# Attention weights asked for among the expert blocks, two blocks turned together, and a new order of work where the experts hand over to self attention

## The chip, the cores and the metric

The kernel runs on one core of one Trainium2 chip. The metric is device time in microseconds for one execution, the median of several runs. All of the work is one launch.

## What is computed

A decoder of two layers for `B = 4` sequences of `S = 512` rows of `D = 256`, with a context of `S2 = 1601` rows for each sequence. After each of its six parts the row is normalized again:

```python
x = _layernorm(x + _L0_attn_ref(x, ...))              # a per-token gradient step, run as attention
x = _layernorm(x + _L0_xattn_ref(x, ctx, ctx, mask, ...))
x = _layernorm(x + _L0_ffn_ref(x, Wr, br, Wi, bi, Wg, bg, Wo, bo, gamma, beta))
x = _layernorm(x + _L1_attn_ref(x, w_qkv, w_out))     # 16 heads of 16, causal
x = _layernorm(x + _L1_xattn_ref(x, ctx, ctx, mask, ...))  # 16 heads, keys and queries turned (rope)
x = _layernorm(x + _L1_ffn_ref(x, ...))               # quantized weights, F = 1024
```

The change touches the third part and the beginning of the fourth. The third is a mixture of `E = 8` experts: for each row the best two of the eight (by `softmax(x @ Wr + br)`) compute

```python
h = gelu(xf @ Wi_e + bi_e) * sigmoid(xf @ Wg_e + bg_e)      # 256 -> 1024
r = xf + (h @ Wo_e + bo_e)                                  # 1024 -> 256
y_e = (r - mu) * rsqrt(var + EPS) * g_e + b_e
```

and the row's result is the sum of its two `y_e` with their weights. The cross attention of the second layer takes turned keys from the context: `K = ctx @ Wk.T + bk`, then `K * cos + swapped(K) * sin`.

## The kernel before

**Engines and order.** TensorE (PE) does the matmuls and the transposes; ScalarE (ACT) does activations and copies out of PSUM; VectorE (DVE) adds, multiplies and reduces; GpSimd (POOL) does a part of the turning, memsets and the indirect DMAs; SyncE (SP) has no arithmetic and issues most DMAs. From the experts on, the program is under a manual schedule (L1146, L1173): each engine carries out its instructions in the order in which the Python code emits them, and an instruction that waits holds all behind it on its engine, a DMA issue too.

**Experts.** Just before the experts, values of the cross attention of the last two sequences are computed and written to the DRAM arrays `vd` (L790 to L794, ACT). The routing scatters each row, normalized, into a DRAM array `xs`, sorted by expert. The rows are computed in blocks of 256: one first block for each of the eight experts (`"first"`, static addresses), and blocks of what is left (`"more"`, two halves of 128 rows, each with an expert found at run time). They run in the order `"ffmfmmfmfmmfmfmmf"` and two more `"m"` (L1138). For one block:

- `rows_of` (L918) loads its 256 rows, `xb`: on SP for a first block (L922, 256 KB), by two indirect DMAs on POOL for another (L928). There are three `xb` buffers.
- `turned` (L933) makes four transposes on PE (L939) and copies them with DVE to `xbT` (L943).
- `first_half` (L946) multiplies by `eWi` (32 matmuls), then by `eWg` (32), with gelu and sigmoid on ACT (L975) and their product on DVE (L977). Between its quarters it asks for `eWi` and `eWg` of the next block: on SP for a first block (L407, 1028 KB each), on POOL for another (L409). There are two buffers of each.
- `second_half` (L982) multiplies by `eWo`, normalizes on DVE (`rb`), writes `ys` (L1012, SP), asks for the rows of the block after the next, and through `outs` for a later `eWo`.

`run` (L1105) strings these together: it asks for the rows of two blocks (`rows_of(b)` for `blocks[:2]`), for the first `eWo`, turns the first block, and then for each block `i`: `first_half(i)`, `turned(i + 1)`, `second_half(i - 1)`, which asks for the rows of `i + 2`. `eWi` and `eWg` of the first two blocks were loaded long before.

**Loads for the attention.** Ahead of all that, L896 to L901 ask for eight weights of 256 KB and four small rows and columns, on SP. In the program they stand in front of `run`, so in SP's queue they stand in front of the first `xb<-xs`. More loads are a generator, `attention_first` (L1019): `run` takes one step of it behind each block. Its steps, in order: masks for the self attention (`c_diagq`, `c_later`, on ACT); context of the first sequence into `qt` and `ks` tiles (L1034, ACT); cosine and sine tables (L1044, ACT); three steps of constant rows written to the DRAM arrays `qd`, `ksd`, `kcd` behind their data (`behind`, L876, ACT; `kcd<-c_rowkc` is the third); memsets on POOL; then four steps that load a piece of the mask on SP (`mi`, L1066), turn it into an addend on DVE (`mf`, L1070) and write it on SP to `mrow` (L1071); `masked(0)` (L879, ACT) copies `mrow` to `kcd[0]`; last come small products of weights (L1091 and after).

**From the experts to the self attention.** In the stage that begins at L1173, emission order again is the order on each engine. The tiles of this stage lie where those of the experts lay; the first load into them is `ln_gamma` (L1575, SP). `combined(b)` returns lists of steps: `fetch` gathers each row's two `ys` rows by indirect DMAs on POOL (L1224); `add` adds them on DVE (L1238) and normalizes the rows, with a root on ACT and an apply; `turn` transposes the rows on PE (L1254) and copies them to `xT` on ACT (L1257). Then `self_rows(b, c)` computes, for half of the heads, k and q (L1271, L1273): a matmul group, an eviction on ACT, a write on SP to `ksd` or `qd` (`to_rows`, L1203), and, in a separate step (`rows0`), the loads of `ks` and `qt` by head groups (`from_rows`, L1206). `self_values` (L1283) computes the values. `context(b, keys, values)` computes keys (`key`, L1325) and values (`value`, L1341) of the cross attention: a key is a matmul group with `xaK`, an eviction on ACT to `raw` (L1332), the turning of `rotated` (L1294; a shuffle on DVE L1298, and three operations on DVE or POOL L1299 to L1301) and a write on SP to `kcd`. There are four `raw` buffers. Values of the second sequence, `values1`, need context chunks `cx`, which `chunk` asks for (L1316, SP, two buffers) one ahead.

The order at this seam was written out by hand at L1773 to L1784: four keys of the first sequence (matmul and eviction, with turning and writing put off to `turns0`), then `add`, then `turns0` (four times turning and writing), three values, `turn`, k and q, `rows0`, four self values, six more values. While these run, `all_banks` is truthy and `one()` (L1187) hands out seven PSUM banks. Behind them the units of the attention start: `slot1` (L1386) computes scores and their row maxima, `subtracted` (L1447) takes the maximum off the queries, `scores` (L1460), `exponents` (L1472) and `weighted` (L1484) follow, with other work (`extras`, `starts`) put between them: `extras[0]` begins with k and q of the second half of the heads, then more keys.

Of the kernel before, what the change touches and what calls it, by code (L numbers as in the profile page):

```python
# [12 lines left out]
AF = mybir.ActivationFunctionType  # L13
# [26 lines left out]
def decoder(ctx: ExitStack, tc: tile.TileContext, a: dict, out: bass.AP):  # L40
    nc = tc.nc
# [33 lines left out]
    def weight(pool, name):  # L75

        src = a[name]
        t = pool.tile([P, 2, src.shape[1]], F32, tag=name, name=name)
        nc.sync.dma_start(t, src.rearrange("(c p) n -> p c n", p=P))
        return t  # L80
# [134 lines left out]
    with (  # L215
# [15 lines left out]
        ps = wide()  # L231
# [661 lines left out]

    with tc.tile_pool(name="p3", bufs=2) as p3, ExitStack() as ordered:
        W = {}
        for name in ("qkvQ", "qkvK", "xaQ", "xaK", "qkvV", "xaV", "outP", "xaO"):  # L896
            W[name] = weight(plw, name)
        bqc = column(plw, "bq")
        bkc = column(plw, "bk")
        bvc = column(plw, "bv")  # L900
        bo_x = row(plw, "xa_bo")  # L901

# [114 lines left out]
        def attention_first():  # L1019

            ready["diagq"] = const(p4a, "c_diagq", [P, 896], nc.scalar)

            later = p3.tile([P, 2 * P], F32, tag="c_later", name="c_later", bufs=1)
            nc.scalar.dma_start(later, a["c_later"])
            ready["later"] = p4a.tile([P, 2 * P], BF16, tag="later", name="later")
            yield
            nc.gpsimd.tensor_copy(ready["later"], later)
            qt, ks = ready["qt"], ready["ks"] = [group_tiles(p4a, n, S) for n in ("qt", "ks")]

            at = qt + ks  # L1030
            for i, k0 in enumerate(range(0, S2, 512)):
                kw = min(512, S2 - k0)
                for h in range(2):
                    nc.scalar.dma_start(at[2 * i + h][:, :kw], a["ctxT"][0, h * P : (h + 1) * P, k0 : k0 + kw])  # L1034
            yield

            for i, k0 in enumerate(range(0, S2, 512)):
                kw = min(512, S2 - k0)
                if i < B - 1:
                    pair = [xT[1 + i][:, h, :] for h in range(2)]  # L1040
                else:
                    pair = [p4a.tile([P, kw], F32, tag=f"turn{h}", name=f"turn{h}") for h in range(2)]
                for t, name in zip(pair, ("c_cos", "c_sin")):
                    nc.scalar.dma_start(t, a[name][:, k0 : k0 + kw])  # L1044
                ready["turn", i] = pair
            yield
            behind(qd[0], "c_rowq")
            behind(ksd[0], "c_rowks")
            yield
            behind(kcd[0], "c_rowkc")  # L1050
            yield
            ngs = ready["ngs"] = []
            for i in range(2 * NT):
                t = p4a.tile([P, 4, 32], F32, tag=f"ng{i}", name=f"ng{i}")
                nc.gpsimd.memset(t, 0.0)
                ngs.append(t)
            ready["vself"] = [values_tile(p4a, f"vs{i}", NT) for i in range(2)]
            yield


            any_ = p3.tile([4 * B, 4], F32, tag="any", name="any", bufs=1)
            for c, k0 in enumerate(range(0, S2, 401)):
                kw = min(401, S2 - k0)
                mi = p3.tile([4 * B, 401], I32, tag="mi", name="mi", bufs=1)[:, :kw]
                for b in range(B):
                    nc.sync.dma_start(  # L1066
                        mi[4 * b : 4 * b + 4, :], a["mask"][b, k0 : k0 + kw].partition_broadcast(4)
                    )
                mf = p3.tile([4 * B, 401], F32, tag="mf", name="mf", bufs=1)[:, :kw]
                nc.vector.tensor_scalar(mf, mi, 0.0, MASKED, ALU.is_equal, ALU.mult)  # L1070
                nc.sync.dma_start(mrow[:, k0 : k0 + kw], mf)  # L1071
                nc.vector.tensor_reduce(any_[:, c : c + 1], mf, AX.X, ALU.max)
                yield
            masked(0)
            yield
            left = p3.tile([4 * B, 1], F32, tag="left", name="left", bufs=1)
            nc.vector.tensor_reduce(left, any_, AX.X, ALU.max)
            nc.vector.tensor_scalar(left, left, 0.0, QS, ALU.is_equal, ALU.mult)
            ones16 = p3.tile([4 * B, P], F32, tag="ones16", name="ones16", bufs=1)
            nc.gpsimd.memset(ones16, 1.0)  # L1080
            dia = p3.tile([4 * B, 4 * B], F32, tag="dia", name="dia", bufs=1)
            nc.vector.tensor_scalar(dia, ident[: 4 * B, : 4 * B], left, None, ALU.mult)
            yield
            ps = bank()
            mm(ps[:, : 4 * B], [(ones16, dia)])
            nc.vector.tensor_copy(live, ps[:, : 4 * B])
            for b in range(B):
                nc.vector.tensor_scalar(liveb[:, b, :], bqc, live[:, 4 * b : 4 * b + 1], None, ALU.mult)
            yield

            ps = bank()  # L1091
            mm(ps[0:1, :D], [(bvc[:, c : c + 1], W["xaO"][:, c, :]) for c in range(2)])
            nc.vector.tensor_tensor(bo_x, bo_x, ps[0:1, :D], ALU.add)
            yield
            ps = bank()
            mm(ps[:, :D], [(ones, bo_x)])
            nc.vector.tensor_copy(bob, ps[:, :D])
# [7 lines left out]
        def run(blocks, work):  # L1105

            get = lambda i: blocks[i] if i < len(blocks) else None
            for b in blocks[:2]:
                rows_of(b)
            for name in ("eWi", "eWg"):  # L1110
                for h in range(2):
                    if (blocks[0], name) not in first_loads:
                        weights_of(blocks[0], name, h)

            ahead = [(b, h) for b in blocks for h in range(len(halves(*b)))]
            taken = [0]

            def outs(free):
                taken[0] -= free
                while ahead and taken[0] < 3:  # L1120
                    b, h = ahead.pop(0)
                    weights_of(b, "eWo", h)
                    taken[0] += 1

            outs(0)
            turned(blocks[0])
            for i, b in enumerate(blocks):
                first_half(b, get(i + 1))
                if get(i + 1):
                    turned(get(i + 1))  # L1130
                if i:
                    second_half(blocks[i - 1], get(i + 2), outs)
                elif get(2):
                    rows_of(get(2))
                next(work, None)
            second_half(blocks[-1], None, outs)
# [30 lines left out]
    with ExitStack() as s4:  # L1167
# [143 lines left out]
        def chunk(n):  # L1311
            while len(chunk_tiles) < min(n + 2, len(stream)):
                b, c = stream[len(chunk_tiles)]
                k0, kw = chunks[c]
                t = p4.tile([P, 2, 512], F32, tag="cx", name="cx", bufs=2)
                nc.sync.dma_start(  # L1316
                    t[:, :, :kw], a["ctxT"][b].rearrange("(c p) k -> p c k", p=P)[:, :, k0 : k0 + kw]
                )
                chunk_tiles.append(t)
            return [chunk_tiles[n][:, h, :] for h in range(2)]  # L1320

        def context(b, keys, values, here=None):


            def key(src, i, c, eng, apart=None):  # L1325
                if apart is None:
                    flush(1)
                k0, kw = chunks[i]
                ps = one()
                mm(ps[:, :kw], [(W["xaK"][:, h, c * P : (c + 1) * P], src()[h][:, :kw]) for h in range(2)])  # L1330
                raw = raw_tile()
                nc.scalar.activation(raw[:, :kw], ps[:, :kw], AF.Identity, bias=bkc[:, c : c + 1])  # L1332
                turn = lambda: rotated(raw, kw, slice(k0, k0 + kw), eng, ready["turn", i] if here else None)
                write = lambda: to_rows(kcd[b], c, k0, kw, raw[:, :kw])
                if apart is None:
                    turn()
                    going.append(write)
                else:
                    apart.append(lambda: (turn(), write()))
# [430 lines left out]
        )  # L1770
        (k1_, q1_), rows1 = self_rows(0, 1)
        turns0 = []
        for f in keys0[0:2] + keys0[4:6]:  # L1773
            f(turns0)
        for f in add + turns0 + values1[:3] + turn + [k0_, q0_, rows0] + self_values(0) + values1[3:9]:
            f()
        all_banks.clear()
        cosT = const(p4c, "c_cos", [P, S2], nc.sync)
# [2 lines left out]

        extras[0] = [
            k1_, q1_, *keys0[2:4], lambda: (keys0[6](), keys0[7]()), lambda: (flush(0), rows1()),
            *values1[9:11],  # L1784
        ] + extras[0]
        extras[1] = values1[11:] + keys1[:2] + extras[1]
        for i, n in enumerate((2, 5)):
# [245 lines left out]
```

## Time and profile before

| | |
|---|---|
| runs, us | 2396.34, 2378.8, 2392.78 |
| median of the runs, us | 2392.78 |
| profiled execution, us | 2391.23 |
| its span, us | 2389.1 |
| mean granted TensorE clock | 0.971 |
| busy, us: PE, PEld, DVE, ACT, POOL | 2270.9, 1287.5, 1231.9, 1063.0, 369.3 |
| instructions | 36156 |
| read from HBM, written, MB | 196.12, 56.77 |

The profile is of one execution. "PEld" is the loading of weights into TensorE, which runs beside the matmuls. In the slices each digit is the busy share of a fortieth of the span in tenths, and PEclk is the granted clock of TensorE. Lines with PE, SPq and so on give start, duration, engine, source line and operation; "SPq", "ACTq" and "POOLq" are issues of DMAs by these engines, "x4" is a count, and square brackets hold the idle time before and what ended it. Lines of waits give the sum, the count and the longest. Rows of windows give the length and then, for each engine, busy time and number of instructions; the last three numbers are the granted clock, the busy share of the DMA engines and GB/s.

### The profile page before, as it was taken

The numbers are of one execution on the slowest core, as the hardware profiler recorded it, in microseconds if no ns is written. First come the engines' busy times: TensorE is split into PE (matmuls) and PEld (weight loads), VectorE is DVE, ScalarE is ACT, GpSimd is POOL, SyncE is SP. The second block draws the span as 40 slices with busy tenths as digits, with TensorE's granted clock in tenths as the row PEclk, the third lists the DMA queues.
The fourth block names the chain that finished last, engine by engine and source line by source line (L and its number), as shares of the span: only waits on it lengthen the run. The fifth ranks groups of instructions, "written<-read, shape, count | busy, mean of one in ns | idle before, by whom it ended". The sixth has DMA issues, their size and how long they took to land.

```text
span 2389.1 us, 36156 instructions
## 1 busy us (share of the span) xinstructions
PE 2270.9 (95%) x14448; PEld 1287.5 (54%) x14448; DVE 1231.9 (52%) x2918; ACT 1063.0 (44%) x2103; POOL 369.3 (15%) x383
## 2 busy tenths in 40 slices
PE   7899999977999999879999999999999999999998
PEld 4768577756888988633333334333333333333366
DVE  1433334431333434455656667666766776777234
ACT  1111222223554645424555443655656565666730
POOL 1010001130222122335230010211112010000000
PEclk9999999988999999989999998999999999999999
DMA  8400311135887767352221310112110010100000
GB/s 302 177 0 1 133 55 46 46 126 190 333 307 269 291 260 297 108 173 85 67 87 54 116 37 1 38 33 72 63 39 28 25 60 15 64 1 21 29 9 27
DMA packets 77099, 244.13 MB, mean 102 GB/s; under 512 B 11640, under 2 KB 34686, under 8 KB 64638
## 3 DMA queue, kind: packets, MB, share of 16 engines
q1 hardware_dynamic: 60126, 141.96, 17.2%
q0 software_dynamic: 13632, 89.32, 9.9%
q10 hardware_dynamic: 3168, 10.48, 1.2%
q8 instruction: 116, 1.90, 0.3%
q14 instruction: 57, 0.47, 0.1%
HBM read 196.12 MB, written 56.77 MB: 106 GB/s over the span
## 4 chain that ended last, share of the span: by engine, by line
PE 53%; ACT 1%; DVE 1%; DMA 1%; POOL 1%; issue 0%; SPq 0%; DVEq 0%; ACTq 0%; POOLq 0%
PE s L1467 23%; PE one L202 12%; PE po L1494 12%; PE s L202 3%; PE s L1477 1%; PE one L1452 1%; PE one L1515 1%; DMA cx<-in_ctxT 1%; ACT x L171 1%; DVE one L1426 0%; ACT ex L1481 0%; DMA y<-ys,yrows 0%; DVE pm L1424 0%; PE one L1536 0%; DMA qd<-q 0%
## 5 line engine op out<-in xcount | busy, mean ns | idle before, releaser
L1481 ACT ACTIVATE ex<-s 128x512 f32<-128x512 f32 (+1 forms) x1062 | 578.0, 594 | 465.5 <-PE s L1467 225.3
L1424 DVE TENSOR_REDUCE pm<-one 128x1 f32<-128x512 f32 x768 | 492.8, 685 | 161.1 <-PE s L1467 106.1
L1467 PE MATMUL s<-q,kc 32*128 32x512 f32 x1612 | 528.8, 639 | 0.8 <-ACT ex L1481 0.8
L202 PE MATMUL one<-kc,qt 32*128 32x512 f32 (+1 forms) x2048 | 483.5, 563 | 0.3 <-DVE pm L1424 0.3
L1467 PEld LDWEIGHTS s<-q,kc 32*128 32x128 f32 x1612 | 166.1, 179 | 203.1 <-issue 170.0
L1494 PE MATMUL po<-ex,v 128*32 128x256 f32 (+3 forms) x2688 | 251.5, 443 | 0.3 <-ACT ot L1507 0.3
L1426 DVE CUSTOM_DVE_ANT_0 one<-one,c_diagq 128x512 f32<-128x512 f32 x256 | 171.9, 715 | 97.8 <-PE one L202 88.2
L1494 PEld LDWEIGHTS po<-ex,v 128*32 128x32 f32 (+1 forms) x2688 | 54.1, 108 | 253.1 <-issue 246.4
L1467 PE MATMUL s<-q,ks 32*128 32x512 f32 x512 | 180.6, 658 | 6.2 <-ACT ex L1481 4.9
L202 PEld LDWEIGHTS one<-kc,qt 32*128 32x128 f32 x2048 | 164.5, 188 | 11.8 <-DVE pm L1424 7.4
L202 PE MATMUL bank<-eWo,g 128*128 128x256 f32 x608 | 140.3, 387 | 11.5 <-DVE rb L997 8.2
L202 PE MATMUL one<-ks,qt 32*128 32x512 f32 x512 | 149.6, 664 | 0.0
L202 PE MATMUL wide<-xbT,eWi 128*128 128x128 f32 (+1 forms) x960 | 141.0, 308 | 4.0 <-DVE xbT L943 4.0
L977 DVE TENSOR_TENSOR g<-g,sg 128x1024 f32<-128x1024 f32 x38 | 46.4, 1224 | 180.3 <-ACT sg L975 171.9
L202 PEld LDWEIGHTS wide<-xbT,eWi 128*128 128x128 f32 x960 | 131.1, 194 | 13.4 <-issue 4.2
L202 PE MATMUL wide<-xbT,eWg 128*128 128x128 f32 (+1 forms) x960 | 137.0, 303 | 0.0
L202 PEld LDWEIGHTS bank<-eWo,g 128*128 128x128 f32 x608 | 115.5, 194 | 31.0 <-DVE rb L997 12.2
L1299 POOL TENSOR_TENSOR raw<-raw,c_cos 128x512 f32<-128x512 f32 (+1 forms) x32 | 35.0, 1093 | 626.5 <-DVE swp L1298 626.5
L202 PEld LDWEIGHTS wide<-xbT,eWg 128*128 128x128 f32 x960 | 128.1, 191 | 6.6
L1467 PEld LDWEIGHTS s<-q,ks 32*128 32x128 f32 x512 | 53.4, 187 | 83.9 <-issue 64.6
L975 ACT ACTIVATE g<-wide,eWi 128x128 f32<-128x128 f32 (+1 forms) x240 | 72.6, 410 | 56.8 <-PE wide L202 56.4
L202 PE MATMUL wide<-ctxT,q 128*128 128x512 f32 (+1 forms) x256 | 91.3, 510 | 0.8 <-DVE q L669 0.8
(346 smaller groups left out, 2948.5 us busy)
## 6 DMA issues: line engine op xcount, KB each, us to landing
xs<-zero SPq DMA_DIRECT2D x32, 512.0 KB
kc<-kcd SPq DMA_DIRECT2D x16, 800.5 KB
eWo<-in_eWo SPq DMA_DIRECT2D x8, 1408.0 KB
eWi<-in_eWi SPq DMA_DIRECT2D x8, 1028.0 KB
eWg<-in_eWg SPq DMA_DIRECT2D x8, 1028.0 KB
qt<-qd SPq DMA_DIRECT2D x32, 256.0 KB
ctxT<-in_ctxT SPq DMA_DIRECT2D x4, 1601.0 KB
cx<-in_ctxT SPq DMA_DIRECT2D x12, 512.0 KB
```

What stands on the lines that cost most here:

```text
L171: nc.scalar.activation(into(t), xb[:, t, :], AF.Identity, scale=mid["rs"][:, t : t + 1], bias=mid["nb"][:, t : t + 1],)
L202: nc.tensor.matmul(ps, l, r, start=(i == 0), stop=(i == n - 1))
L975: nc.scalar.activation(dst[:, k, :], pv[:, k, :], func, bias=bias)
L977: nc.vector.tensor_tensor(part, part, dst, ALU.mult)
L1299: eng.tensor_tensor(raw[:, :n], raw[:, :n], cos[:, :n], ALU.mult)
L1424: nc.vector.tensor_reduce(pm[:, t, j, c : c + 1], ps, AX.X, ALU.max)
L1426: nc.vector.tensor_tensor_reduce(out=ps, in0=ps, in1=diagq[:, 384 - t * P : 896 - t * P], scale=1.0, scalar=LOWEST, op0=ALU.add, op1=ALU.m ...
L1452: nc.tensor.transpose(pt[:, t * P : (t + 1) * P], ng.rearrange("p j r -> p (j r)"), ident)
L1467: nc.tensor.matmul(ps[:kn], kt[rows, k * P : k * P + kn], q2[rows, :], start=True, stop=cross)
L1477: nc.tensor.matmul(ps[:, k * P : (k + 1) * P], later_[:, :P], later_[:, P:], start=False, stop=True)
L1481: nc.scalar.activation(ex[:kn, h, :], ps[:kn], AF.Exp)
L1494: nc.tensor.matmul(state["po"][j * 32 : j * 32 + 32, q0:q1], (vals if cross else vself)[b % 2][:kn, k, c0 : c0 + 32], ex[:kn, j % 2, q0:q1 ...
```

## The change

The loads of the attention weights leave the place in front of the experts. They are put into two steps of the generator: four weights and the small loads at the start of its second step, four weights at the start of its seventh, ahead of the first piece of the mask. The names `bqc`, `bvc` and `bo_x` are bound there.

```diff
         W = {}
-        for name in ("qkvQ", "qkvK", "xaQ", "xaK", "qkvV", "xaV", "outP", "xaO"):
-            W[name] = weight(plw, name)
-        bqc = column(plw, "bq")
-        bkc = column(plw, "bk")
-        bvc = column(plw, "bv")
-        bo_x = row(plw, "xa_bo")
+
+        def attention_weights(names):
+            for name in names:
+                W[name] = weight(plw, name)
...
             ready["later"] = p4a.tile([P, 2 * P], BF16, tag="later", name="later")
             yield
+            attention_weights(("xaV", "xaK", "qkvK", "qkvQ"))
+            for name in ("bq", "bk", "bv"):
+                ready[name] = column(plw, name)
+            ready["xa_bo"] = row(plw, "xa_bo")
             nc.gpsimd.tensor_copy(ready["later"], later)
...
             ready["vself"] = [values_tile(p4a, f"vs{i}", NT) for i in range(2)]
             yield
+            attention_weights(("qkvV", "xaQ", "outP", "xaO"))
+            bqc, bvc, bo_x = (ready[k] for k in ("bq", "bv", "xa_bo"))
```

The first two blocks are turned one after the other, ahead of the first block's matmuls; until now the second was turned behind the first half of the first:

```diff
             outs(0)
-            turned(blocks[0])
+            for b in blocks[:2]:
+                turned(b)
             for i, b in enumerate(blocks):
                 first_half(b, get(i + 1))
-                if get(i + 1):
+                if i and get(i + 1):
                     turned(get(i + 1))
```

At the seam, two of the four keys precede `add` and a third follows it; then come the transposes of `x`, k and q, the fourth key, and the loads of the finished rows. Turning and writing of the four keys stand behind all of these. Eight values follow instead of nine, the ninth going to `extras[0]`. The context chunks asked for meanwhile go to ACT's queue:

```diff
-                nc.sync.dma_start(
+                (nc.scalar if all_banks else nc.sync).dma_start(
                     t[:, :, :kw], a["ctxT"][b].rearrange("(c p) k -> p c k", p=P)[:, :, k0 : k0 + kw]
                 )
...
-                nc.scalar.activation(raw[:, :kw], ps[:, :kw], AF.Identity, bias=bkc[:, c : c + 1])
+                nc.scalar.activation(raw[:, :kw], ps[:, :kw], AF.Identity, bias=ready["bk"][:, c : c + 1])
...
         turns0 = []
-        for f in keys0[0:2] + keys0[4:6]:
-            f(turns0)
-        for f in add + turns0 + values1[:3] + turn + [k0_, q0_, rows0] + self_values(0) + values1[3:9]:
+        apart = lambda f: lambda: f(turns0)
+        order = [apart(f) for f in keys0[0:2]] + add + [apart(keys0[4])] + turn + [k0_, q0_, apart(keys0[5]), rows0]
+        for f in order:
+            f()
+        for f in turns0 + self_values(0) + values1[:8]:
             f()
         all_banks.clear()
...
-            *values1[9:11],
+            *values1[8:11],
```

No arithmetic is added or left out.

## The prediction

> **What bounds the kernel now.** I read the slices first, then what TensorE (PE) waits for, then the two places where it stops.
>
> ```profile
> PE   7899999977999999879999999999999999999998
> PEclk9999999988999999989999998999999999999999
> DMA  8400311135887767352221310112110010100000
> ```
>
> A slice is 59.7 us. PE is full nearly everywhere, so the end is set by PE's work plus its holes. Two dips lie at the stages that the diff touches: slices 9 and 10 (experts begin) and 17 and 18 (experts end, attention begins). The waits of PE in 545:600 and in 1000:1040 name both:
>
> ```profile
> PE bank L939 <- DMA xb<-xs: 19.0, 1, 19.0
> PE wide L202 <- DVE xbT L943: 4.0, 2, 3.2
> PE one L202 <- DMA cx<-in_ctxT: 11.3, 1, 11.3
> ```
>
> The timeline of the first hole (start, duration, engine, line; brackets: idle before, and what ended it):
>
> ```profile
> 531.37 0.37 SPq L79 DMA_DIRECT2D qkvQ<-in_qkvQ  x1
> 542.89 1.08 SPq L922 DMA_DIRECT2D xb<-xs  x2
> 546.00 1.09 PE L939 MATMUL bank<-ident,xb 128*128 128x128 f32 x4 [18.98 <-DMA xb<-xs]
> 547.92 9.06 PE L202 MATMUL wide<-xbT,eWi 128*128 128x256 f32 x32 [0.84 <-DVE xbT L943]
> 567.50 8.83 PE L202 MATMUL wide<-xbT,eWi 128*128 128x256 f32 x32 [3.17 <-DVE xbT L943]
> 576.17 7.07 PE L202 MATMUL wide<-xbT,eWg 128*128 128x256 f32 x32
> ```
>
> SP is free at 531.37, but issues twelve attention loads before the rows that PE waits for. And the second:
>
> ```profile
> 1013.07 9.37 SPq L1203 DMA_DIRECT2D kcd<-raw  x4
> 1022.55 0.58 SPq L1203 DMA_DIRECT2D ksd<-q  x1
> 1028.95 0.34 SPq L1206 DMA_DIRECT2D qt<-qd  x1
> 1030.34 0.93 SPq L1316 DMA_DIRECT2D cx<-in_ctxT  x2
> 1036.51 2.05 PE L202 MATMUL one<-xaV,cx 128*128 128x256 f32 x4 [11.30 <-DMA cx<-in_ctxT]
> 1038.49 2.06 PE L202 MATMUL one<-ks,qt 32*128 32x512 f32 x8
> ```
>
> SP holds the finished k and q behind four writes of turned keys (9.4 us); the next context chunk, which PE's order has ahead of the first scores, stands behind both.
>
> **Experts begin.** The first xb load takes the place of qkvQ. In the built order it waits for the same things (the vd writes, behind which qkvQ went at 531.37) and the last scatter (issued 519.27, long done). So it issues at 531.4. Its landing is the row's 546.00 - 542.89 = 3.1 us: PE starts at 534.5. Both blocks are turned, 2 x 1.1 at the clock of that place; the first expert matmul comes at 536.7 instead of 547.92: **-11.2**. Unknown is the landing of the second xb, beside POOL's eWo (issued 532.26): 2 to 5 us for both, so -9 to -12. Then, before the second block, the turn (0.6) and the wait for its DVE copy (3.17) go: **-3.8**.
>
> The third part is the clock, and here a rule is weighed. Two-us rows of the granted clock (the column behind the engines):
>
> ```profile
> 550.00:552.00 2.00, 2.00 (x6) 1.61 (x6) 0.00 (x0) 0.00 (x0) 0.00 (x0) 0.56 1.00 408
> 552.00:554.00 2.00, 2.00 (x11) 1.76 (x10) 0.00 (x0) 0.43 (x2) 0.00 (x0) 1.00 0.55 231
> ```
>
> After the long idle PE runs at half clock until about 551.8, 5.8 us after its first transpose. The Trainium skill (TensorE: Matmul & The Clock Gate, "What's actually happening") says half clock after one idle window of about 3.4 us, and full clock after one busy window as long. By the rule a cold start costs 3.4/2 = 1.7, by the row 2.9. PE is idle from 527 to 534.5 in the changed kernel too, so the first cold start stays and gains nothing by either. The 3.17 us hole is under the rule's window, so the rule gives it no clock loss; the row does: eWi of the second block takes 8.83 where its eWg takes 7.07 for the same 32 matmuls. I take the row: **-1.8** (rule: 0). Sum -16.8.
>
> **The weights in the stage of experts.** Two groups of four (1 MB each, plus four small loads in the first), twelve SP issues of about 0.5, now stand between expert loads. From 600 to 955 the DMA rows show 0.77 busy at 293 GB/s, so 2 MB (7 us at that rate) fit in volume. What matters is the order on SP. Group one goes behind the rows of the fourth block and ahead of that block's eWi and eWg. In the built order bq waits for the landing of those rows (a completion semaphore shared with the DMA eight before). A rule and a row differ again:
>
> ```profile
> 596.30 0.76 SPq L922 DMA_DIRECT2D xb<-xs  x1
> 600.66 0.35 SPq L407 DMA_DIRECT2D eWi<-in_eWi  x1
> 607.02 0.63 PE L939 MATMUL bank<-ident,xb 128*128 128x128 f32 x4 [2.15 <-DMA xb<-xs]
> 614.39 7.07 PE L202 MATMUL wide<-xbT,eWi 128*128 128x256 f32 x32
> ```
>
> The skill (DMA: Bandwidth & Descriptors, "Anatomy of one DMA") gives a fit, made for POOL's descriptors, of about 2.0 us + bytes/436 GB/s: 2.6 for these 256 KB if it held on SP, and eWi would hardly be held. The row says 10.7 in full queues. By the row, eWi goes at about 609 instead of 600.66; with 1 MB at about 350 GB/s and the 2 us it lands near 614, when PE asks. Cost 0 (rule) to 2; and eWg, needed 7 us later, nothing. On ACT the qt/ks loads wait for one landing more (1 to 2 us), under PE's 2.15 us wait for xb. Group two goes ahead of the mask loads (SP at 708.3), which the DVE awaits at 715.43 in front of the gate product, and SP's next eWi (716.31) stands behind that. PE needs that eWi at 725.43: 9 us of slack against four issues (2) and 1 MB (3 to 5). 0 to 6 in all for both groups; I take **+1.5**. Net of the first two edits: -15.3.
>
> **Experts end.** On ACT only two instead of four key evictions (L1332, 0.57 from start to start) precede the root: -1.2 at 1009.56. Of what came between the applied rows and the xT copies (three values), one key is left. So the k matmul moves from 1013.75 to 1012.7. From there PE's order is k and q 3.6, the last key 1.7, four self values 3.4, eight values 6.9 (0.86 each): scores at 1028.3. k and q are written at about 1015 and 1017, not behind the turned keys; q needs 5.7 to come back (1023.22 to 1028.95) and its load about 3: 1026, under PE's values. So scores start at 1028.3 instead of 1038.49: -10.2. The ninth value is done later: +0.9. The first slot loses its half clock: about -0.4. The first two cx loads on ACT must wait, as ln_gamma on SP did, until 991.98; behind them stand value copies that began at 989.82, 3 us late, while PE has seven banks to fill: 0. The third waits on ACT for qt's landing, with four copies behind it: 0 to 1. The DVE turns the same four keys to about 1022 either way; their writes now go behind the rows, and raw tiles come free some 3 us later against the next keys. The mask write behind row constants (13 us from 1034.47) stands ahead of k and q of the second half: 0 to 3. I take +0.7 for these. Sum **-9.0** (range -5 to -12).
>
> **Total** -24.3. From 1130 on PE is full, so it is kept. The profiled execution took 2391.2 (span 2389.1), 1.6 under the median of the runs: 2366.9 beside it, 2368.5 beside the median 2392.8.
>
> **Rivals.** *Experts give it back*: the weights' small rows share the engines badly with expert loads; both eWi come 5 us late and the mask holds the gate product. For: 10.7 us for 256 KB, and mask loads already cost PE 3.3 us near 745. Against: 9 us of slack and DMA at 0.77. -24.3 + 9 = -15: 2377.
>
> *The seam's wait moves*: scores start early, but the third and fourth head groups' rows stand behind the mask write and POOL's turns (1050.90 to 1060.4), and PE waits there. For: four turns on POOL at 3.8 us each are a chain that PE can't shorten. Against: that chain starts with PE's own key matmuls, so it shifts along. -15.3 - 2: 2375.
>
> *Slower*: the second weights hold mask loads, mask holds DVE, and SP's eWi stands behind the mask's write. Up to 9 us it is free; then every us is PE's. It would eat 24.3 from a delay of 33 us; at 45 the kernel takes 2405. A 256 KB load took 10.7; four in a row at that pace are 43. Against: POOL's loads beside them end by 720, so they can't stay that slow.
>
> **How the numbers follow.** Likeliest, both holes close: 0.55, 2361 to 2376 on its own. Experts give back: 0.2. Seam moves: 0.19. Slower: 0.06. The runs of before already spread from 2378.8 to 2396.3. 8 in 10: 2354 to 2384. A measurement of this kernel can tell about 1%, 2368.9 here, and the likeliest case lies on that edge: half of it, and a part of the spread, is faster by over 1% (0.42); the rest of it and the next two cases are within 1% (0.52); slower 0.06.
>
> **What would show it.** xb<-xs on SP near 531; the first transpose near 534.5; no wait between the first two blocks; second hole gone, scores some 26 us earlier than 1038.49, qd<-q ahead of kcd<-raw. Wrong would be: PE waiting for eWi near 614 or 725 (less the shift), DVE for the mask longer than 8 us, PE waiting on ks or qt after its values.

## The result and the profile after

The changed kernel takes 2363.88 us (median of 5 runs, 2360.89 to 2369.97) beside 2389.59 for the kernel before: ratio 0.9904, 95% interval 0.9883 to 0.9924, or 25.7 us less. In a second series, beside 2385.96, it took 2356.62: ratio 0.9883 (0.9866 to 0.9900). The profiled execution has a span of 2367.9 (2389.1 before).

The slices of the changed kernel, of 59.2 us each:

```profile
PE   7899999989999999889999999999999999999998
PEclk9999999989999999889999988999999999999999
DMA  8400311127877777343131210111110010101000
```

The first dip is shallow now: 8 and 9 in slices 9 and 10, where 7 and 7 stood. The second is hardly shallower: 8 and 8 in slices 17 and 18 for 8 and 7. The waits of PE in 525:600 and in 1000:1060 (sum, count, longest) say why:

```profile
PE bank L937 <- DMA xb<-xs: 6.4, 1, 6.4
PE wide L202 <- ACT g L973: 2.1, 1, 2.1
PE s L1472 <- DVE q L1461: 7.2, 1, 7.2
```

The wait for the first rows fell from 19.0 to 6.4 us and that for the second block's turn is gone. The wait for `cx` is gone too, but PE now waits 7.2 us for `q`, where it waited 1.3. The begin of the experts in the changed kernel's timeline:

```profile
530.20 0.88 SPq L920 DMA_DIRECT2D xb<-xs  x2
533.08 1.94 PE L937 MATMUL bank<-ident,xb 128*128 128x128 f32 x8 [6.41 <-DMA xb<-xs]
535.00 8.43 PE L202 MATMUL wide<-xbT,eWi 128*128 128x256 f32 x32
550.17 7.07 PE L202 MATMUL wide<-xbT,eWi 128*128 128x256 f32 x32
```

Both row loads are first on SP, the eight transposes run together, and the two blocks follow without a hole: first expert matmul 12.9 us earlier than 547.92, second block 17.3 earlier than 567.50. And the seam, from k's write to the first scores with `q`:

```profile
994.84 0.71 SPq L1208 DMA_DIRECT2D ksd<-q  x1
1001.72 0.33 SPq L1211 DMA_DIRECT2D qt<-qd  x1
1003.09 3.60 SPq L1208 DMA_DIRECT2D kcd<-raw  x4
1008.35 1.14 PE L202 MATMUL one<-ks,qt 32*128 32x512 f32 x8
1011.27 0.60 SPq L876 DMA_DIRECT2D kcd<-in_c_rowkc  x1
1027.02 0.51 SPq L879 DMA_DIRECT2D kcd<-mrow  x1
1027.62 0.65 SPq L1208 DMA_DIRECT2D ksd<-raw  x1
1031.84 0.32 ACT L1337 ACTIVATE raw<-s,bk 128x65 f32<-128x65 f32 x1 [8.93 <-DMA ksd<-raw]
1032.29 0.23 DVE L1303 STREAM_SHUFFLE swp<-raw 128x65 f32<-128x65 f32 x1
1033.78 0.68 DVE L1461 TENSOR_TENSOR q<-qt,s 128x512 f32<-128x512 f32 x1
1034.61 1.19 PE L1472 MATMUL s<-q,ks 32*128 32x512 f32 x1 [7.16 <-DVE q L1461]
```

The first five lines are what the change was meant to give: k and q written ahead of the turned keys, scores at 1008.35, 30.1 us earlier than in the kernel before. The other six are a chain, read upwards from the last: PE waits for `q`; DVE has it behind the shuffle of a short key; ACT could not evict that key for 8.9 us, since the `raw` tile was still being written to `ksd`; and that write stood on SP behind the mask copy, which went out 15.8 us behind the row constants, since it waits for their landing.

**A ledger over all profiles.** The stretch before the experts differs from profile to profile (last value matmul there at 517 to 527), so I measure from landmarks: A, the end of those values; V, the first value matmul of the next stage (`s<-xaV,qt`); Q, the first scores with `q` (`s<-q,ks`); U, the transposed maxima of the fourth unit of the attention (`s<-` or `one<-ident,ng`). "First scores" are the first `one<-ks,qt`. Time in us, each worked out from that kernel's one profile:

| kernel | A to V | V to first scores | V to Q | V to U | median, before beside it | ratio, 95% |
|---|---|---|---|---|---|---|
| before | 461.1 | 50.3 | 71.4 | 143.9 | | |
| changed | 440.5 | 41.2 | 67.5 | 143.2 | 2363.88, 2389.59 | 0.9904, 0.9883 to 0.9924 |
| changed, again | 441.1 | 37.2 | 62.5 | 139.3 | 2356.62, 2385.96 | 0.9883, 0.9866 to 0.9900 |
| e1_front | 441.4 | 49.5 | 70.8 | 143.6 | 2365.19, 2383.16 | 0.9919, 0.9899 to 0.9940 |
| e2_seam | 458.5 | 37.4 | 63.7 | 139.9 | 2375.13, 2383.16 | 0.9969, 0.9958 to 0.9980 |
| e3_weights | 446.0 | 49.2 | 71.8 | 145.0 | 2369.34, 2383.16 | 0.9945, 0.9924 to 0.9965 |
| e4_turn | 454.6 | 49.5 | 71.0 | 143.8 | 2378.04, 2383.16 | 0.9979, 0.9970 to 0.9989 |
| e5_mask | 445.1 | 41.7 | 64.8 | 141.9 | 2366.72, 2390.48 | 0.9903, 0.9881 to 0.9925 |
| e6_cxsp | 438.5 | 40.6 | 68.0 | 144.5 | 2366.42, 2390.48 | 0.9905, 0.9884 to 0.9927 |
| e7_key4 | 441.0 | 39.5 | 67.3 | 142.6 | 2365.60, 2390.48 | 0.9905, 0.9884 to 0.9927 |
| e8_eight | 459.4 | 45.0 | 67.6 | 144.4 | 2387.35, 2390.48 | 0.9989, 0.9972 to 1.0005 |
| e9_late | 447.9 | 37.1 | 57.4 | 132.6 | 2352.64, 2385.96 | 0.9858, 0.9838 to 0.9877 |
| e10_late_key4 | 442.3 | 35.9 | 58.8 | 135.0 | 2354.48, 2385.96 | 0.9874, 0.9857 to 0.9891 |
| e11_seam_late | 459.7 | 39.8 | 60.1 | 137.8 | 2374.55, 2385.96 | 0.9955, 0.9938 to 0.9972 |

From U to the end all take 1251.7 to 1257.6, without order by the edits.

### The profile page after: what moved, and what is told of

Same layout as the page of the kernel before. It is cut to its first block, busy times and chain, and to the rows that moved or that the text cites. A ratio compares the mean times of both kernels' runs of the same rounds, so it can differ in the third digit from the quotient of the medians.

```text
span 2367.9 us, 36132 instructions
## 1 busy us (share of the span) xinstructions
PE 2271.9 (96%) x14440; PEld 1287.9 (54%) x14440; DVE 1233.4 (52%) x2918; ACT 1064.2 (45%) x2103; POOL 371.2 (16%) x383
## 4 chain that ended last, share of the span: by engine, by line
PE 54%; DMA 1%; DVE 1%; ACT 1%; POOL 1%; SPq 0%; issue 0%; DVEq 0%; POOLq 0%; ACTq 0%
PE s L1472 24%; PE one L202 12%; PE po L1499 12%; PE s L202 3%; PE s L1482 1%; PE one L1457 1%; DMA kcd<-in_c_rowkc 1%; PE one L1520 1%; ACT x L171 0%; ACT ex L1486 0%; DMA y<-ys,yrows 0%; DMA cx<-in_ctxT 0%; DVE pm L1429 0%; DVE one L1431 0%; PE one L1541 0%
## 6 DMA issues: line engine op xcount, KB each, us to landing
kc<-kcd SPq DMA_DIRECT2D x16, 800.5 KB
```

## The experiments

My theory after the result: the begin of the experts gave nearly all, and the seam gave little, since its new order uncovered a transfer. The rivals: both parts gave what was forecast and something later took it; or the wait for `q` is DVE's own.

**One half alone.** e1_front has the weights and the two blocks of the change, and the old seam:

```diff
-            turned(blocks[0])
+            for b in blocks[:2]:
+                turned(b)
...
-                if get(i + 1):
+                if i and get(i + 1):
...
+            attention_weights(("xaV", "xaK", "qkvK", "qkvQ"))
...
+            attention_weights(("qkvV", "xaQ", "outP", "xaO"))
```

> The weights moved among the expert blocks and two blocks turned together; the seam as before. If the two halves of the change add up: first expert matmul near 535.0 us, the second block's near 550.2, the experts' last eWo matmuls near 959.5 (980.5 before), then the seam of before with its 11.3 us wait for cx, so about -21 us, some 2369. If the gain of the experts' begin is lost again where the experts end (rival: the seam waits for something that does not move with PE), the wait for cx grows to over 20 us and the time is within 5 us of before. The 3.3 us wait for DVE near block 11 (mask): absent if the order of the weights removed it, present if it was chance.

Measured: 18.0 us under before. A to V is 441.4, that of the changed kernel; `cx` is waited for 11.2 us, as before. The gain is not lost where the experts end.

e2_seam has the other half:

```diff
-        for f in keys0[0:2] + keys0[4:6]:
-            f(turns0)
-        for f in add + turns0 + values1[:3] + turn + [k0_, q0_, rows0] + self_values(0) + values1[3:9]:
+        order = [apart(f) for f in keys0[0:2]] + add + [apart(keys0[4])] + turn + [k0_, q0_, apart(keys0[5]), rows0]
+        for f in order:
             f()
+        for f in turns0 + self_values(0) + values1[:8]:
...
-                nc.sync.dma_start(
+                (nc.scalar if all_banks else nc.sync).dma_start(
```

> Only the order at the seam, with the cx loads on ACT's queue; the weights and the first blocks as before. If my ledger is right: last eWo matmuls at about 980.5 as before, first scores about 9.1 us earlier than the 1038.5 of before, then a wait of about 7 us for DVE's q ahead of the first scores with q2 (1.3 before), so -3 to -5 us in all, some 2386. Rival (the wait for q comes only from the earlier experts of the full change): no such wait, -9, some 2381. Near block 11 the 3.3 us wait for DVE is there again if it belongs to the order of before.

Measured: 8.0 us under before (ratio: 4.8 to 10.0). First scores come 12.9 us earlier behind V, and the wait for `q` is there, 7.2 us, with the experts of before: it belongs to the seam's order. V to U is 4.0 shorter; the rest of the 8.0 lies in stretches that the edit doesn't touch, and I don't credit it.

**The front, taken apart.** e3_weights moves the weights and leaves the second block's turn in its place:

```diff
             outs(0)
-            for b in blocks[:2]:
-                turned(b)
+            turned(blocks[0])
...
-                if i and get(i + 1):
+                if get(i + 1):
```

> Only the weights moved; the second block is turned behind the first half of the first, as before. By the rows of before: first expert matmul near 534.5, the 3.2 us hole ahead of the second block is there and its eWi takes 8.8 instead of 7.1 (the clock row), so 12.3 earlier at the second block's end and about -16 in all, some 2374. By the rule of the clock[...]: hole 3.2, eWi 7.1, about -18.

e4_turn does the reverse: the edit of `run` alone, with the weights still ahead of the rows.

```diff
-            turned(blocks[0])
+            for b in blocks[:2]:
+                turned(b)
...
-                if get(i + 1):
+                if i and get(i + 1):
```

> Only the two blocks turned together, with the weights still ahead of the first rows on SP. First transpose near 546 as before, both blocks turned in about 2, first expert matmul 1 us later than the 547.9 of before, no hole ahead of the second block and its eWi at 7.1: second block's eWi 4 us earlier than the 567.5 of before, at 563.5; with the clock -5 in all, some 2386. Rival: the second xb lands later than the first by more than 1 us and the first matmul waits for it, so that 2 us or less remain.

Measured: 13.8 and 5.1 us under before (by the intervals 8.3 to 18.1 and 2.6 to 7.1, so the time of e3_weights doesn't tell its two forecasts apart); their sum, 18.9, is that of e1_front within its interval. The second block's first matmuls in e2_seam, whose experts are those of before, and in e3_weights:

```profile
562.67 7.14 PE L202 MATMUL wide<-xbT,eWi 128*128 128x256 f32 x32 [3.17 <-DVE xbT L943]
```

```profile
553.21 7.14 PE L202 MATMUL wide<-xbT,eWi 128*128 128x256 f32 x32 [3.17 <-DVE xbT L941]
```

The same hole of 3.17 us, and full speed behind it: 7.14, not the 8.83 of before's profile. Of five profiles with this hole, two show 8.8 (before, e11_seam_late) and three 7.1 (e8_eight is the third). The row that I preferred to the rule was one throw of two: in the same code the loss comes and goes. In e4_turn:

```profile
542.80 1.94 PE L939 MATMUL bank<-ident,xb 128*128 128x128 f32 x8 [19.31 <-DMA xb<-xs]
560.53 7.07 PE L202 MATMUL wide<-xbT,eWi 128*128 128x256 f32 x32
```

PE waits 19.3 us for the rows, as before, and the second block follows the first at once: the second row load did not come later.

**The wait for q.** e5_mask takes the mask copy out of SP's way:

```diff
-        rows_behind(1, True, True)
+        rows_behind(1, True, False)
+        behind(kcd[1], "c_rowkc", nc.sync)
+        starts[1].append(lambda: masked(1, nc.sync))
```

> The changed kernel, with one step moved: the copy of the second sequence's mask row to kcd goes from the end of the seam to the head of the second unit of the self attention; its row constants stay. If the 7.2 us wait for DVE's q is the chain constants (15 us in flight) - mask copy waiting on SP - k and q writes behind it - raw tiles held - ACT's key eviction - DVE's shuffle - q, the wait falls to the 1.3 us of before or less and the time is 5 to 6 us under the changed kernel's, some 2352 beside a before of 2383. Rival: the wait is DVE's and POOL's own turning, or PE waits the same time for something behind it; then the time stays at 2358.

Measured: ratio 0.9903, no different from the changed kernel (0.9904), so the 5 to 6 us did not come, and 4.0 of the 7.2 us stay. Its timeline:

```profile
1018.95 0.65 SPq L1208 DMA_DIRECT2D ksd<-raw  x1
1032.53 0.32 ACT L1337 ACTIVATE raw<-s,bk 128x65 f32<-128x65 f32 x1 [5.89 <-DMA ksd<-raw]
1035.19 1.19 PE L1472 MATMUL s<-q,ks 32*128 32x512 f32 x1 [4.03 <-DVE q L1461]
```

k's write now goes out at 1018.95, ahead of any mask copy, but its tile is not free before 1032.5: it is in flight for 13.6 us, behind the turned keys, tables and row constants issued on SP just before. From the first of these writes (`kcd<-raw`) to the free tile it is 24.7 us here (1007.86 to 1032.53) and 28.8 in the changed kernel (1003.09 to 1031.84). So SP's wait was one part of the cause, and what is in front on the queue another. In e9_late the constants of `kcd` move with the copy:

```diff
-        rows_behind(1, True, True)
+        rows_behind(1, True, False)
+        starts[4].append(lambda: rows_behind(1, False, True))
```

> The changed kernel with the second sequence's row constants of kcd and the mask copy behind them moved from the end of the seam to the head of the fifth unit. Moving the copy alone left 4.0 of the 7.2 us: the k and q writes then went early but stayed in flight 13 us, behind 1.6 MB of constants and the tables. If it is this transfer, the wait for DVE's q falls to 1.3 or less and the first scores with q2 come 5 to 6 us earlier than in the changed kernel (67.5 us behind the first value copied from the context; then 61 to 62). Rival: the two tables (1.6 MB) in front do the same alone; then 4 us stay. By the time: some 6 us under the changed kernel run beside it.

```profile
1006.11 0.65 SPq L1208 DMA_DIRECT2D ksd<-raw  x1
1018.43 0.32 ACT L1337 ACTIVATE raw<-s,bk 128x65 f32<-128x65 f32 x1 [1.48 <-PE s L202]
1022.70 1.09 PE L1472 MATMUL s<-q,ks 32*128 32x512 f32 x2 [1.21 <-DVE q L1461]
```

ACT waits for PE again and not for the tile (free within 21.5 us of the first `kcd<-raw`, at 996.91), PE waits 1.2 us, and V to Q is 57.4: 5.1 under the changed kernel run beside it, and V to U 6.7 under it. By the time it is 4.0 under that one (its runs 2343.73 to 2355.85, those of the changed kernel 2355.95 to 2357.91), the fastest of all. e11_seam_late puts both edits of `e2_seam` and `e9_late` on the kernel before:

> The kernel before with the new order at the seam and the late row constants; weights and first blocks as before. The seam alone brought first scores 9 to 13 us earlier and lost 7 of it to the wait for q. Without that wait: first scores with q2 at 58 to 59 us behind the first value (71.4 before), so 11 to 13 us under before; rival: 7 to 8 as with the seam alone.

Measured: V to Q 60.1, 11.3 under before, and 11.4 us by the time; V to U is only 6.1 under before. The rival (7 to 8) is at the interval's edge (7 to 15), but the trace shows the wait gone: 1.2 us. No run moved the constants alone in the kernel before, gave `raw` a fifth buffer, or put these writes on another queue.

**Parts of the seam.** e6_cxsp undoes the queue of the `cx` loads:

```diff
-                (nc.scalar if all_banks else nc.sync).dma_start(
+                nc.sync.dma_start(
```

> The changed kernel with the cx loads back on SP. The eight values need the first two chunks alone, which are asked for long before; the third stands behind four kcd writes, at about 1006.7 instead of 1005.0, and is used in extras only. So no difference beyond 1 us if dropping the ninth value took away the wait for cx; rival: without ACT's queue PE waits again for cx, up to 11 us, and the time goes back to some 2367.

Measured: 0.9905, no difference in time, and no wait for `cx` at the seam. V to U is 1.4 and 5.2 longer than in the changed kernel's two profiles, with a hole of 3.6 us ahead of the transposes (2.1 and 0.5 there), so a loss of an us or two is not excluded. e8_eight is the kernel before with the ninth value put off:

```diff
-... + self_values(0) + values1[3:9]:
+... + self_values(0) + values1[3:8]:
...
-            *values1[9:11],
+            *values1[8:11],
```

> The kernel before with one edit: eight values of the second sequence instead of nine ahead of the attention, the ninth in extras. PE then does not wait for the third cx chunk at the seam, but for ks and qt, whose loads go at 1027.4 to 1029.0 and take about 3 us: scores at 1032 instead of 1038.5, so -6 if this single value is most of the gain of the seam; rival: qt and ks stay the bound at 1037 or later, or the third chunk is missed a little later in extras, and -2 or less remain.

```profile
1030.26 2.09 PE L202 MATMUL one<-ks,qt 32*128 32x512 f32 x8 [8.75 <-DMA qt<-qd]
```

First scores come 5.3 us earlier behind V, now waiting for `qt`; the wait for `cx` was the ninth value's. But V to U is 144.4, as before, and the time unchanged (0.9972 to 1.0005): a gain at the first scores that is gone by the fourth unit, here without a wait for `q` (1.5 us). Where it goes is told below, under "Experts end". e7_key4 puts the fourth key ahead of the transposes, and e10_late_key4 does so with late constants:

```diff
-... add + [apart(keys0[4])] + turn + [k0_, q0_, apart(keys0[5]), rows0]
+... add + [apart(keys0[4]), apart(keys0[5])] + turn + [k0_, q0_, rows0]
```

> The changed kernel with the fourth key ahead of the transposes of x. Its 1.7 us of matmuls fill the hole of 2.1 us ahead of the transposes, and if that hole brought the half clock from 988 to 995, k's matmuls take 1.98 instead of 3.78; ACT copies one key more ahead of xT, 0.6 later. Between -2.5 (hole and clock gone) and +0.6 (neither was worth anything) against the changed kernel.

> As e9_late, and the fourth key ahead of the transposes. With the fourth key alone first scores came 1.7 us earlier, but the wait for q took it all back (8.7 for 7.2). If the wait's cause is gone here, the 1.7 us stay: 7 to 8 us under the changed kernel; rival: they are lost again, and it equals e9_late.

Measured: nothing in the time of either (0.9905; 0.9874 beside e9_late's 0.9858). In e7_key4 first scores came 1.7 us earlier than in the changed kernel's first profile, but 2.3 later than in its second, and the wait for `q` grew to 8.7. The hole ahead of the transposes shrank to 0.5 us, yet k's matmuls took 3.2 instead of 1.98: that hole is not the only thing that brings the half clock there. In e10_late_key4 the wait for `q` is 3.8, with ACT waiting for k's write again: PE comes earlier, but the tile is free 21.0 us behind the first `kcd<-raw` (992.20 to 1013.20), no sooner than in e9_late. The rival was right, and the queue is still the bound.

**The control**, the changed kernel once more:

> The changed kernel once more, as a control beside these: 23 to 26 us under before; the 7 to 8 us wait for q at the first unit, no 3.3 us wait for DVE near block 11. How long TensorE stays at half clock at the start of the first unit with turned keys (some 19 us in before, 28 in the changed kernel) differs from run to run if it is chance, and is 28 again if the change made it.

Measured: 29.3 us under before, more than I expected. The wait for `q` is there (6.2 us), no wait of 3.3 near block 11, and the half clock in the first unit with turned keys is the long one again (27.3 us). But it is long too in e11_seam_late, which has the experts of before, and short (20.5) in e5_mask and e2_seam: it does not follow the change. The 2.1 us hole and the half clock at the seam's transposes, which the changed kernel's first profile shows, are absent here: V to first scores is 37.2, not 41.2.

## Why the prediction was right, and where its steps were not

**The total.** -24.3 was forecast, -25.7 measured. The ledger gives A to V -17.5 (mean of eight profiles with the new front, 442.2, against four with that of before, 459.7) and V to U -3.3 (changed, again and e2_seam, mean 140.8, against four with the old seam, 144.1): -20.8, where the steps had -15.3 and -9.0. The interval of the time, 18.2 to 28.0, holds both numbers, and the two profiled executions differ by 21.2. So that the total came within 1.4 us is in part luck: the gain up to V was forecast 2.2 too small, that of the seam 5.7 too large, and the other 4.9 of the 25.7 are not in the stretches that the edits touch (the runs of before alone spread over 17.5 us).

**Experts begin: right.** -16.8 forecast; 18.0 by e1_front's time with all of the front. The rows went out at 530.2 (531.4 forecast), the first transposes came at 533.1 (534.5), and the first expert matmul 11.9 us earlier behind A on the mean of eight profiles with the new front and four with the old (11.2 forecast). -3.8 for the second block's turn held: in e4_turn that block starts 37.0 us behind A, 3.7 earlier than on the mean of the four (40.7). The clock's -1.8 was mis-sized: it is 0 or 1.7 by chance, as three and two profiles show, so less than half on the mean.

**Weights in the stage: +1.5 forecast, not told from 0.** From the second block's `eWi` to V the nine profiles with moved weights take 415.0 to 423.6 us (mean 417.9), the five without 417.4 to 420.6 (mean 418.7). What I named is there: ACT held by the `ks` loads (PE waits 2.1 us for `g`, in place of the wait for `xb`), the mask's first piece 5 us late, `eWi` behind it up to 1.3 late. The sign that I had named as wrong, DVE waiting longer than 8 us for the mask, came too: 13.0, where before had 8.0. It cost PE little: it waits 0.95 us for that `eWi`, as most of the 5 us are within the slack. What I had not seen is that the wait for the next piece of the mask shrinks. Before, the first piece's use, then DMA issue and use of the second:

```profile
715.43 0.36 DVE L1070 TENSOR_SCALAR mf<-mi 16x401 f32<-16x401 int32 x1 [7.98 <-DMA mi<-in_mask]
732.03 1.56 SPq L1066 DMA_DIRECT2D mi<-in_mask  x4
734.37 0.94 POOL L409 DMA_INDIRECT eWi<-in_eWi,wrow  x1 [4.00 <-ACT g L975]
742.41 0.36 DVE L1070 TENSOR_SCALAR mf<-mi 16x401 f32<-16x401 int32 x1 [11.39 <-DMA mi<-in_mask]
```

And in the changed kernel:

```profile
702.52 0.36 DVE L1074 TENSOR_SCALAR mf<-mi 16x401 f32<-16x401 int32 x1 [12.97 <-DMA mi<-in_mask]
714.13 1.46 SPq L1070 DMA_DIRECT2D mi<-in_mask  x4
717.65 0.94 POOL L409 DMA_INDIRECT eWi<-in_eWi,wrow  x1 [5.17 <-ACT g L973]
722.32 0.36 DVE L1074 TENSOR_SCALAR mf<-mi 16x401 f32<-16x401 int32 x1 [9.21 <-DMA mi<-in_mask]
```

Counted from the mask's issue PE is 1.2 us later there, so POOL asks for a big load 3.5 instead of 2.3 us behind the mask, and DVE has the mask 8.2 instead of 10.4 us after its issue. All five profiles without moved weights have PE waiting for DVE there, 3.15 to 3.45 us; of nine with them five have no such wait, three have 0.8 to 1.6, and one, e9_late, has 3.3. That POOL's load is the cause is argued from these lines; I made no run for it.

**Experts end: the step that failed.** First scores were forecast 10.2 us earlier and came 9.1 earlier behind V, and 13 where no hole of 2 us and half clock came in between. Means of the ledger against the four profiles with the old seam:

| profiles | first scores | Q | U |
|---|---|---|---|
| new seam, constants in place (changed, again, e2_seam) | -11.0 | -6.7 | -3.3 |
| new seam, late constants (e9_late, e10_late_key4, e11_seam_late) | -12.1 | -12.5 | -9.0 |

So the first term held; two behind it were mis-sized. The first is: "The mask write behind row constants ... stands ahead of k and q of the second half: 0 to 3. I take +0.7 for these." It costs 5.7: V to U is 140.8 with these constants where they are, and 135.1 with them moved. By the time it is less, 2.1 to 4.0 (e10_late_key4 and e9_late against the changed kernel; 3.4 for e11_seam_late against e2_seam, each beside its own before). I had read the chain's end right for SP, but sized it as if the landing moved along with PE. It does not: ahead of k's write SP has issued, after the turned keys, two tables of 800.5 KB, two sets of row constants of 512 KB and these of 1601 KB, 4.2 MB in all. In the kernel before the first 5 us of this transfer ran under PE's 11.3 us wait for `cx`, which ended at 1036.51:

```profile
1031.32 0.66 SPq L861 DMA_DIRECT2D c_cos<-in_c_cos  x1
1034.47 0.59 SPq L876 DMA_DIRECT2D kcd<-in_c_rowkc  x1
1040.48 1.98 PE L202 MATMUL s<-xT,qkvK 128*128 128x512 f32 x4
1048.38 0.50 SPq L879 DMA_DIRECT2D kcd<-mrow  x1
1049.01 0.65 SPq L1203 DMA_DIRECT2D ksd<-raw  x1
1059.55 1.25 PE L1467 MATMUL s<-q,ks 32*128 32x512 f32 x2 [1.30 <-DVE q L1456]
```

PE's k for the second half stands 9.2 us behind the first of these issues there. In the changed kernel it stands 2.7 behind it (1009.42 and 1006.73), and PE has to wait. Closing the hole took the transfer's cover away. And I had the wait at `ks` and `qt` of later head groups, while it went by `raw` tiles, ACT and DVE to `q` of the first.

The second mis-sized part is the ninth value and the clock, +0.9 and -0.4, so 0.5 together. From Q to U all ten profiles with eight values at the seam take 75.2 to 77.7 us, the four with nine 72.5 to 73.2: 3.4 more, whether the constants are moved or not. The stretch from Q to U in before, in e8_eight, whose one edit is this value, and in e9_late:

```profile
1059.55:1132.08 72.53, 69.16 (x394) 26.58 (x394) 42.88 (x133) 34.81 (x67) 29.39 (x32) 0.93 0.29 87
```

```profile
1052.84:1129.59 76.75, 72.12 (x391) 27.72 (x391) 42.99 (x133) 35.11 (x68) 30.84 (x34) 0.89 0.30 86
```

```profile
1022.70:1097.89 75.19, 71.11 (x391) 27.12 (x391) 43.02 (x133) 35.11 (x68) 30.13 (x33) 0.91 0.30 86
```

The matmuls differ by that one value alone (0.9 us); beside it 16 products for `po` of 256 columns become 8 of 512, the same work. What differs is the granted clock, 0.93 in the four profiles and 0.89 to 0.91 in the ten. What the clock lacks of full speed, times the length, is 5.1 us in each of the four and 6.8 to 8.7 in the ten (mean 8.0), which is 2.9 of the 3.4. It is also where e8_eight, 3.8 ahead at Q, comes to be 0.4 behind at U. Why the clock is lower there stays open. So that the seam is worth the forecast's -9.0 with late constants is luck: first scores came earlier than forecast, and this loss took it back.

**The rivals.** "The seam's wait moves" happened in kind, though not at that place. "Experts give it back" did not. The slower one needed a delay of 33 us of the second weights; they delayed the mask's first piece by 5.

## What to carry to other kernels

Before a hole counts as gain, list which transfers run in it and who needs their landing: the hole may be their cover, and then it is paid later, at an engine that does not look related. A write that frees a tile counts as a wait of the engine that needs the tile, and moving its issue ahead helps only in part while megabytes are in front on the same queue (7.2 us of wait became 4.0). Compare at several landmarks: a gain at the first can be gone at the next. A stall or a slow group that one profile shows is one throw: look for it in a second profile before it gets a place in a sum.

## What the runs showed of the hardware

TensorE was at half clock for some time at the start of the first unit with turned keys in all fourteen profiles, though no gap of PE there is over 0.3 us: for 20.5 us in six (before, e1_front, e2_seam, e4_turn, e5_mask, e8_eight), 23.9 in two (e6_cxsp, e7_key4) and 27.3 in six (changed, again, e3_weights, e9_late, e10_late_key4, e11_seam_late). Windows of before, and of the changed kernel at the same work (length; busy time and count of PE, PEld, DVE, ACT, POOL; clock, DMA, GB/s):

```profile
1445.00:1455.00 10.00, 10.00 (x61) 6.40 (x61) 7.25 (x15) 0.62 (x2) 0.00 (x0) 0.61 0.01 2
```

```profile
1420.30:1430.30 10.00, 10.00 (x57) 6.67 (x53) 7.29 (x14) 0.60 (x1) 0.00 (x0) 0.50 0.01 2
1430.30:1440.30 10.00, 10.00 (x50) 2.44 (x46) 4.50 (x9) 4.04 (x7) 1.52 (x2) 0.75 0.00 0
```

It starts, at 1432.4 in before, while PE has only score matmuls of 32 rows, back to back:

```profile
1428.73 20.62 PE L202 MATMUL one<-kc,qt 32*128 32x512 f32 x80 [0.27 <-DVE pm L1424]
```

No run tried what brings it, and the length does not follow the edits (e1_front and e3_weights have the same seam and the same moved weights). The lengths are 3.4 us apart, which is the window that the Trainium skill gives for this clock (TensorE: Matmul & The Clock Gate, "What's actually happening"). 6.8 us at half clock should cost 3.4; from the 16th to the 19th unit the profiles with the shortest take 153.0 to 153.4 us, the two between them 154.6 and 154.7, and those with the longest 156.2 to 156.5. The page ties the half clock to windows in which PE idles; here it came with PE busy.
